# One of seven products in a weight product, split once more, in a two-layer cross-attention kernel

## The chip, the core and the metric

The kernel runs on one core of a Trainium2 chip. The metric is the device time of one execution in microseconds (us), lower being better. In the profile the core's engines are PE (matrix multiplication; PEld is its weight load), DVE (elementwise work and reductions), ACT (one function per element, here mostly copies, scaled copies and exponentials), POOL (here mostly the issue of transfers that add to their destination) and SP (the issue of plain loads). PE multiplies `lhs.T @ rhs` into banks of PSUM; everything else lies in SBUF. Each engine works through its own instructions in order and waits for the others by semaphores.

## The reference

Two cross-attention layers, one after the other, on `x` (8 x 100 x 1024) with a context of 8 x 1444 x 512. The first layer is, in essence:

```python
Q = query @ Wq + bq
K = key @ Wk + bk
V = key @ Wv + bv
weights = softmax(Q @ K.T / sqrt(1024))
x = query + (weights @ V) @ Wo + bo
```

The second layer has the same queries, keys and values with weights of its own, no output projection, and a layer norm on the sum. Everything is in float32.

## The kernel before

The scores `Q K.T` are rearranged so that the context is never projected: `Wq Wk.T` is one matrix of 1024 x 512, made first; the queries are multiplied by it, and the result meets the context directly. Likewise `Wv Wo` is one matrix. Each of the three weight products (`qk0` and `vo0` for the first layer, `qk1` for the second) is made by `weight_products`, with its sum over 1024 rows. The order is `qk0`, `vo0`, the first layer's queries, `qk1`, then the attention of the eight batches, twice.

`weight_products` cuts both factors into 2 x 2 blocks and makes the product of blocks by seven products in place of eight: sums of blocks are made first (S1 to S4 of the left factor, T1 to T4 of the right one), and the seven results are added into the four blocks of the output. With A and B for the blocks, the seven are: A11 B11 and A12 B21; S1 T1 (the variable Y); S2 T2, which goes on in the banks of A11 B11 (X); A22 T4 (W); S3 T3, again on X's banks; and S4 B22. In `qk0` each is 16 matmuls of 128 x 128 weights and 256 columns: four chunks of rows, each in two banks of PSUM with two blocks of columns. `inner_product` does the same once more inside one of the seven: seven smaller products of 4 matmuls with 128 columns. In `qk0` the last of the seven (`Q`) is made like that, and alternated with the one before it; `half_steps` gives the matmuls of a product one at a time, so that two can be taken in turn. In `vo0` and `qk1` (the variable `deep`) the product S1 T1 is split too, and alternated with S2 T2.

Values move by three helpers. `put` copies banks of PSUM to the output block by ACT. `add` adds a bank to it by DVE. `combine` makes the sums of blocks by DVE, one instruction for each of four chunks. Several of the sums overwrite their inputs: in `qk0` S2 is written over S1, and S3 over A21. The banks of X are copied out for block (0, 1) after S2 T2, before S3 T3 goes on in them.

PE's order is the order of the program, written out by hand. The other engines' orders come from a scheduler, except for instructions marked to stay in the order of the program; `vector.in_order = True` marks DVE's.

Beside the product each stage makes two bias vectors. `accumulate(0)` makes `bk`'s product with the left factor, 1024 wide, as a sum of eight terms, one for each chunk of rows. For `qk0`, `transferred_sum` makes the first four terms as scaled copies by ACT (`scaled_copies`, line 633) and adds them up in pairs by adding transfers that POOL issues (`transfer_added`, line 628). The second four are made by DVE in one tile, `prob1`, by one scaling and three multiply-adds (`second_half`), and a transfer adds the tile. `accumulate(1)` makes `bq`'s product with the right factor, 512 wide, by eight instructions of DVE.

The inputs of all weight products lie in a pool of ten tiles (`unit`). `vo0` needs eight of them, and only two are free during `qk0`, so SP's loads for `vo0` from its third on wait until a tile of `qk0` is read for the last time. The tiles `prob0` to `prob2` and the tiles of tags `row`, `wT` and `gT` are shared by the stages as room for sums.

Of the kernel before, what the change touches and what calls it, by code (L numbers as in the profile page):

```python
# [25 lines left out]
F32 = mybir.dt.float32  # L26
AF = mybir.ActivationFunctionType
ALU = mybir.AluOpType
# [3 lines left out]
P = 128  # L32
# [25 lines left out]
def two_layer_cross_attention(ctx: ExitStack, tc: tile.TileContext, a: dict, out: bass.AP):  # L58
# [32 lines left out]
    def wide_sums(name):  # L91
        return work.tile([P, LC, GT], F32, tag="gT", name=name, bufs=3).rearrange("p c t -> p (c t)")
# [70 lines left out]
    def half_steps(banks, lhs, rhs, fresh, nb, width):  # L163

        lhs, rhs = singles(lhs), singles(rhs)
        per = nb // len(banks)
        for i in range(len(lhs)):
            for n in range(nb):
                nc.tensor.matmul(  # L169
                    banks[n // per][:, n % per * width : (n % per + 1) * width],  # L170
                    lhs[i][:, n * P : (n + 1) * P],
                    rhs[i],
                    start=(fresh and i == 0 and n % per == 0),
                    stop=(i == len(lhs) - 1),
                    skip_group_check=True,
                )
                yield
# [8 lines left out]
    def combine(to, x, y, op, engine=vector):  # L186
        for t, p, q in zip(to, x, y):
            engine.tensor_tensor(t, p, q, op)
# [164 lines left out]
    def weight_products(name, left, right, l_width, r_width, scaled, between=None):  # L353
# [32 lines left out]

        accs = {}

        def accumulate(side):
            for v, of in scaled:  # L390
                if of != side:
                    continue
                width = (l_width, r_width)[side]
                first = 0 if side == 0 else l_width
                srcs = [(units[h][:, first : first + width], cols[v][:, h : h + 1]) for h in range(EC)]
                if width == E:
                    accs[v] = transferred_sum(f"{name}_{v}", srcs, name)
                    continue
                acc = work.tile([P, L], F32, tag="half", name=f"{name}_{v}", bufs=1)
                accs[v] = acc  # L400
                if early:
                    tiles = [acc] + [t[:, i * L : (i + 1) * L] for t in prob for i in range(2)]
                    scaled_sum(tiles + [weight_rows(f"{name}_{v}_7")[:, :L]], srcs)
                    continue
                for h, (src, by) in enumerate(srcs):
                    if h == 0:
                        vector.tensor_scalar(acc, src, by, None, ALU.mult)
                    else:
                        vector.scalar_tensor_tensor(acc, src, by, acc, ALU.mult, ALU.add)
# [20 lines left out]
        def pair(n):  # L430
            return [(bank2 if n == "w" else bank)(f"{name}_{n}{j}") for j in range(2)]

        def product(banks, lhs, rhs, fresh):
            half_product(banks, lhs, rhs, fresh, nb, rh)

        def block(r, c, j):

            n = r * nb + j * per
            return dst[:, n : n + per, c * rh : (c + 1) * rh]

        def put(r, c, banks):
            for j in range(2):
                nc.scalar.copy(block(r, c, j), banks[j].rearrange("p (n w) -> p n w", n=per))  # L443

        def add(r, c, banks):
            for j in range(2):
                to = block(r, c, j)
                vector.tensor_tensor(to, to, banks[j].rearrange("p (n w) -> p n w", n=per), ALU.add)
# [47 lines left out]
        if name == "qk0":  # L496

            t2, t4 = (weight_rows(f"{name}_t{n}") for n in (2, 4))
            T2, T4 = ([t[:, i * rh : (i + 1) * rh] for i in range(H)] for t in (t2, t4))
            Z = pair("z")  # L500
            product(Z, A12, B21, True)
            combine(T2, B22, T1, ALU.subtract)
            combine(T4, B21, T2, ALU.subtract)
            combine(S1, A21, A22, ALU.add)
            add(0, 0, Z)
            accumulate(1)
            W = pair("w")
            product(W, A22, T4, True)
            accumulate(0)
            put(1, 0, W)  # L510
        elif not deep:
            combine(S1, A21, A22, ALU.add)
            Z = pair("z")
            product(Z, A12, B21, True)
            accumulate(0)
        t = wide_sums(f"{name}_t")
        if deep:

            T2, S2, T4 = B11, A11, B21
            first, rest = slice(0, H - 1), slice(H - 1, H)  # L520
            combine(S1[first], A21[first], A22[first], ALU.add)
            for some in (first, rest):
                if some is rest:
                    combine(S1[some], A21[some], A22[some], ALU.add)
                combine(B12[some], B22[some], B12[some], ALU.subtract)
                combine(T2[some], B22[some], T1[some], ALU.subtract)
            Z = pair("z")
            product(Z, A12, B21, True)
            next(side, None)
            combine(A21, A11, A21, ALU.subtract)  # L530
            combine(S2, S1, A11, ALU.subtract)
            V = half_steps(X, S2, T2, False, nb, rh)
            for n, _ in enumerate(inner_product(f"{name}_y", S1, T1, nb, rh, t[:, 768:1536], *parts(1, 1))):
                run(islice(V, 2 * nb // (2 if n == 1 else 4)))
                if n == 1:
                    add(0, 0, Z)
                elif n == 3:
                    combine(T4, B21, T2, ALU.subtract)
                if n > 2:
                    next(side, None)  # L540
            run(V)
            put(0, 1, X)
        else:
            Y = pair("y")
            product(Y, S1, T1, True)
            put(1, 1, Y)
            vector.in_order = name != "qk0"
            combine(B12, B22, B12, ALU.subtract)
            if name != "qk0":
                T2, T4 = B11, B21  # L550
                combine(T2, B22, T1, ALU.subtract)
                add(0, 0, Z)
            combine(S1, S1, A11, ALU.subtract)
            S2 = S1
            combine(A21, A11, A21, ALU.subtract)
            if name != "qk0":
                combine(T4, B21, T2, ALU.subtract)
            product(X, S2, T2, False)
            put(0, 1, X)
        vector.in_order = True  # L560
        if name == "qk0":
            accs[scaled[0][0]][1]()
        V = half_steps(X, A21, B12, False, nb, rh)
        _, more = parts(0, 1)

        def last():
            combine(A12, A12, S2, ALU.subtract)
            if deep:
                for j in range(2):
                    to = block(0, 1, j)  # L570
                    vector.tensor_tensor(to, to, block(1, 1, j), ALU.add)
            else:
                add(0, 1, Y)
            return inner_product(f"{name}_q", A12, B22, nb, rh, t[:, 768:1536], more, more)

        if name == "qk0":
            run(islice(V, 2 * nb))
# [21 lines left out]
    def transferred_sum(name, srcs, of):  # L599

        n = EC if of == "qk1" else EC // 2
        tiles = [row(f"{name}_{n}") for n in range(2)] + [weight_rows(f"{name}_2")[:, :E]]
        tiles += [t[:, :E] for t in prob]
        if of != "qk0":
            tiles += [weight_rows(f"{name}_{n}")[:, :E] for n in range(6, 8)]
        if of == "qk1":
            tiles = [tiles[i] for i in (0, 3, 1, 4, 2, 5, 6, 7)]  # L610
        scaled_sum(tiles[:n], srcs[:n])

        def second_half():
            t = tiles[n]
            if of != "qk0":
                scaled_sum(tiles[n:], srcs[n:])
            else:
                for i, (src, by) in enumerate(srcs[n:]):
                    if i == 0:
                        vector.tensor_scalar(t, src, by, None, ALU.mult)  # L620
                    else:
                        vector.scalar_tensor_tensor(t, src, by, t, ALU.mult, ALU.add)
            transfer_added(tiles[0], t)

        return tiles[0], second_half

    def transfer_added(to, t):
        nc.gpsimd.dma_start(out=to, in_=t, accum_op=ALU.add)
# [6 lines left out]
    def scaled_sum(tiles, srcs, levels=None):  # L635

        scaled_copies(tiles, srcs)
        k = 1
        while k < len(tiles) and (levels is None or k < 2**levels):
            for i in range(0, len(tiles) - k, 2 * k):  # L640
                transfer_added(tiles[i], tiles[i + k])
            k *= 2
# [1032 lines left out]
```

## Time and profile before

| What | us |
|---|---|
| median of three runs | 574.87 (574.80 to 577.21) |
| the profiled execution | 574.70 |
| its span, first to last instruction | 572.8 |
| first matmul of `qk0` to the last | 4.57 to 52.35 |
| matmuls of `vo0` | 52.49 to 98.39 |
| DVE's last idle time before `qk0`'s sums | 8.5 to 13.41 |
| one 128x1024 scaled copy on ACT | 1.13 |
| one 128x1024 multiply-add on DVE | 1.28 |
| issue of an adding transfer on POOL | 0.86 to 0.91 |

The span is what the profiler saw between the first and the last instruction; the execution's time has 1.9 us more around it. Lines of a timeline give the start and the length of a group of instructions in us, then the engine, the line of the kernel, the operation, the tile written and the tiles read, the shapes and the count; in square brackets stands the engine's idle time before the group, and what ended it. Tiles that differ by a number in their names are put together, so `qk` stands for the inputs and the output of a query/key product, `qk_x` for X's banks, `qk_L_xattn_bk` for rooms of the key bias. In the table of stretches each engine has its busy time and its count of instructions; the last three columns are PE's granted clock, the share of the 16 DMA engines that was busy, and GB/s. In the shares of DMA queues q0 carries the transfers that POOL issues, q1 the loads that SP issues, each with packets, MB and its share of the 16 engines' time.

### The profile page before, as it was taken

What the parts mean: (1) busy time and instruction counts of PE and PEld (TensorE: products, weight loads), DVE (VectorE), ACT (ScalarE), POOL (GpSimd) and SP (SyncE); (2) the same over time, 40 slices, a digit from 0 to 9 for tenths busy, and PEclk for the clock granted to TensorE, in tenths of its full rate; (3) what the DMA queues carried; (4) which work ended last, traced back from release to release, by engine and by line L of the source; (5) the groups of instructions that cost most, each with busy time, mean ns of one, the idle gap of its engine ahead of it and who ended that gap; (6) DMA issues with size and microseconds to landing.
All of it is one profiled execution on the core that took longest, in us unless ns stands there. A gap on an engine that the chain in (4) does not pass through costs nothing.

```text
span 572.8 us, 17296 instructions
## 1 busy us (share of the span) xinstructions
PE 561.9 (98%) x7316; PEld 470.5 (82%) x7316; DVE 447.5 (78%) x1035; ACT 146.0 (25%) x383; POOL 112.9 (20%) x171
## 2 busy tenths in 40 slices
PE   9999999999999999999999999999999999999995
PEld 8887567678999999998997856678999869859672
DVE  1997979879989794876368687896688779979865
ACT  1331321356020112211111000123333035336633
POOL 3110110223100042242222000000421312404232
PEclk9999999999999999999999999999999999999999
DMA  8959979949929998999998003985799989985804
GB/s 283 315 112 327 313 191 291 317 85 206 208 57 348 378 353 323 355 374 340 333 355 275 3 1 141 280 291 189 233 311 305 314 265 330 311 261 168 211 15 92
DMA packets 73389, 141.23 MB, mean 247 GB/s; under 512 B 8160, under 2 KB 29920, under 8 KB 73312
## 3 DMA queue, kind: packets, MB, share of 16 engines
q1 hardware_dynamic: 66592, 121.40, 61.8%
q0 software_dynamic: 6288, 18.20, 16.3%
q8 instruction: 58, 0.95, 0.7%
q10 hardware_dynamic: 432, 0.52, 0.3%
q14 instruction: 19, 0.16, 0.1%
HBM read 123.49 MB, written 6.03 MB: 226 GB/s over the span
## 4 chain that ended last, share of the span: by engine, by line
PE 95%; issue 2%; DVE 1%; POOL 1%; ACT 1%; DVEq 0%; POOLq 0%
PE s L1076 22%; PE A L1004 21%; PE qk_x L169 7%; PE g_x L169 6%; PE vo_x L169 4%; PE o_x L169 3%; PE g_y L169 3%; PE o_x L1327 3%; PE qk_z L169 2%; PE o_y L1327 2%; PE o_y L169 1%; PE qk_w L169 1%; PE qk_y L169 1%; PE vo_z L169 1%; PE qk_q_x L169 1%
## 5 line engine op out<-in xcount | busy, mean ns | idle before, releaser
L1004 PE MATMUL A<-w,c 128*64 128x100 f32 (+2 forms) x3072 | 217.9, 250 | 1.0 <-issue 1.0
L1004 PEld LDWEIGHTS A<-w,c 128*64 128x64 f32 (+2 forms) x3072 | 191.6, 137 | 4.8 <-issue 2.8
L1076 PE MATMUL s<-g0T,cT 128*64 128x100 f32 (+1 forms) x1472 | 109.3, 250 | 1.3 <-issue 1.3
L1076 PE MATMUL s<-g1T,cT 128*64 128x100 f32 (+1 forms) x1472 | 109.6, 249 | 0.0
L1076 PEld LDWEIGHTS s<-g0T,cT 128*64 128x64 f32 (+1 forms) x1472 | 95.5, 136 | 1.7 <-issue 1.4
L1076 PEld LDWEIGHTS s<-g1T,cT 128*64 128x64 f32 (+1 forms) x1472 | 95.3, 136 | 1.1 <-DMA cT<-in_ctxT 0.6
L1294 POOL TENSOR_TENSOR part<-w 128x500 f32<-128x500 f32 x16 | 25.3, 1582 | 238.5 <-DVE rtotal L101 75.8
L1272 ACT ACTIVATE w<-w,negmax 128x100 f32<-128x100 f32 x96 | 34.9, 365 | 44.8 <-DVE negmax L101 44.5
L1140 ACT ACTIVATE w<-w 128x400 f32<-128x400 f32 (+2 forms) x32 | 12.7, 446 | 116.8 <-DVE w L101 106.1
L101 DVE STREAM_TRANSPOSE z<-xT 32x256 f32<-32x256 f32 x88 | 38.3, 436 | 1.4
L169 PE MATMUL qk_x<-qk 128*128 128x256 f32 x160 | 37.8, 380 | 0.0
L169 PEld LDWEIGHTS qk_x<-qk 128*128 128x128 f32 x160 | 28.9, 191 | 3.4 <-ACT qk L443 0.2
L1057 DVE RECIPROCAL rrow<-A 128x100 f32<-128x100 f32 x8 | 6.1, 767 | 23.9 <-PE A L1048 23.9
L169 PE MATMUL vo_x<-vo 128*128 128x512 f32 x48 | 23.3, 594 | 0.0
L101 DVE TENSOR_REDUCE most<-s 128x100 f32<-128x400 f32 (+1 forms) x24 | 12.5, 524 | 10.9 <-PE s L1076 10.4
L101 DVE SCALAR_TENSOR_TENSOR w<-s,kb 128x400 f32<-128x400 f32 (+2 forms) x32 | 14.1, 463 | 8.2 <-PE s L1076 7.8
L101 DVE TENSOR_TENSOR w<-w,rtotal 128x400 f32<-128x400 f32 (+2 forms) x32 | 18.1, 567 | 1.1
L1272 ACT ACTIVATION_READ_ACCUMULATOR w<-w,negmax 128x1 f32 x96 | 17.9, 187 | 0.0
L739 ACT ACTIVATE g1T<-g_x,k 128x400 f32<-128x400 f32 x4 | 2.4, 593 | 60.5 <-PE g_x L169 60.3
L1297 POOL TENSOR_TENSOR part<-part 128x100 f32<-128x100 f32 x32 | 15.8, 493 | 2.5
L101 DVE TENSOR_TENSOR qk<-qk 128x256 f32<-128x256 f32 (+2 forms) x26 | 14.4, 580 | 0.0
L169 PE MATMUL qk_z<-qk 128*128 128x256 f32 x64 | 14.1, 379 | 0.0
(484 smaller groups left out, 1001.1 us busy)
## 6 DMA issues: line engine op xcount, KB each, us to landing
c<-in_ctx SPq DMA_DIRECT2D x176, 256.0 KB, 5.7
cT<-in_ctxT SPq DMA_DIRECT2D x96, 176.0 KB, 4.9
cT<-in_ctxT SPq DMA_DIRECT2D x32, 370.0 KB, 6.2
cT<-in_ctxT SPq DMA_DIRECT2D x32, 352.0 KB, 6.1
cT<-in_ctxT SPq DMA_DIRECT2D x32, 194.0 KB, 5.5
vo<-in_L_xattn_Wo SPq DMA_DIRECT2D x8, 512.0 KB, 9.1
qk<-in_L_xattn_WqT SPq DMA_DIRECT2D x8, 512.0 KB, 5.8
qk<-in_L_xattn_WqT SPq DMA_DIRECT2D x15, 256.0 KB, 5.3
```

What stands on the lines that cost most here:

```text
L101: ins = getattr(nc.vector, op)(*args, **kw)
L169: nc.tensor.matmul(banks[n // per][:, n % per * width : (n % per + 1) * width], lhs[i][:, n * P : (n + 1) * P], rhs[i], start=(fresh and i ...
L739: nc.scalar.activation(dst[g][:, c, :], banks[j][:, :GT], AF.Identity, bias=u[:, c : c + 1])
L1004: nc.tensor.matmul(ps[h * HP : (h + 1) * HP, k * T : (k + 1) * T], block[rows, m % CQ, k * P + h * HP : k * P + (h + 1) * HP], s["w"][rows ...
L1057: nc.vector.reciprocal(r, ps[:, GT : GT + T])
L1076: nc.tensor.matmul(to, cT[k][:, o : o + n], q[:, k, t0 : t0 + T], start=(k == 0 and m % GM == 0), stop=(k == LC - 1 or (k == LC - 2 and no ...
L1140: nc.scalar.activation(rows, rows, AF.Exp)
L1272: ins = nc.scalar.activation(rows[:, i, :], rows[:, i, :], AF.Exp, bias=negmax[:, i : i + 1], accum_out=total[:, i : i + 1])
L1294: add(part, w[:, 0:5, :], w[:, 5:10, :], ALU.add)
L1297: add(part[:, 0, :], part[:, 0, :], more, ALU.add)
L1327: nc.tensor.matmul(ps[:n, :], lhs[0][:, i, :], rhs[0][:, i, :], start=(fresh and i == 0), stop=(i == 1), skip_group_check=True,)
```

## The change

In `qk0` the product S1 T1 is now made by `inner_product`, as in the other two stages, and its steps alternate with the matmuls of S2 T2: two of the 16 after each of the seven steps, four after the second. For this S2 is no longer written over S1, but into two tiles of tag `gT`, and the last product's sums get a third one. DVE keeps the order of the program from here on. The result of S1 T1 goes to block (1, 1) in parts, by `put` and `add`; where it was added to block (0, 1) from PSUM, the finished block (1, 1) is now added.

`accumulate(1)` is cut in two: its first four terms stay where they were, the second four come after the fifth small product, between the difference for T3 and the one for S3.

The second four terms of the key bias are now four scaled copies by ACT, in three steps that are set off during the small products, and adding transfers: the fifth term into `prob1` (t) and the sixth into `prob2` (u), u added to t; the seventh into `prob0` (v); the eighth into u again; then u added to v, v to t, and t to the sum of the first four. That is seven adding transfers in all, where there were four.

```diff
-        def accumulate(side):
+        def accumulate(side, some=range(EC)):
...
-                acc = work.tile([P, L], F32, tag="half", name=f"{name}_{v}", bufs=1)
-                accs[v] = acc
+                if some[0] == 0:
+                    accs[v] = work.tile([P, L], F32, tag="half", name=f"{name}_{v}", bufs=1)
+                acc = accs[v]
...
-                for h, (src, by) in enumerate(srcs):
+                for h in some:
+                    src, by = srcs[h]
...
-            accumulate(1)
+            accumulate(1, range(H))
             W = pair("w")
             product(W, A22, T4, True)
             accumulate(0)
             put(1, 0, W)
...
         else:
-            Y = pair("y")
-            product(Y, S1, T1, True)
-            put(1, 1, Y)
-            vector.in_order = name != "qk0"
-            combine(B12, B22, B12, ALU.subtract)
...
-            combine(S1, S1, A11, ALU.subtract)
-            S2 = S1
-            combine(A21, A11, A21, ALU.subtract)
...
-            product(X, S2, T2, False)
-            put(0, 1, X)
+            vector.in_order = True
+            late = accs[scaled[0][0]][1]()
+            rooms = [wide_sums(f"{name}_s2_{i}") for i in range(2)]
+            S2 = [t2[:, i * lh : (i + 1) * lh] for t2 in rooms for i in range(2)]
+            combine(S2, S1, A11, ALU.subtract)
+            Y = inner_product(f"{name}_y", S1, T1, nb, rh, t[:, 768:1536], *parts(1, 1))
+            V = half_steps(X, S2, T2, False, nb, rh)
+            for n, _ in enumerate(Y):
+                run(islice(V, 2 * nb // (2 if n == 1 else 4)))
+                if n in (1, 2, 5):
+                    next(late)
+                if n == 3:
+                    combine(B12, B22, B12, ALU.subtract)
+                elif n == 4:
+                    accumulate(1, range(H, EC))
+                    combine(A21, A11, A21, ALU.subtract)
+            run(V)
+            put(0, 1, X)
         vector.in_order = True
-        if name == "qk0":
-            accs[scaled[0][0]][1]()
...
         def last():
             combine(A12, A12, S2, ALU.subtract)
-            if deep:
-                for j in range(2):
-                    to = block(0, 1, j)
-                    vector.tensor_tensor(to, to, block(1, 1, j), ALU.add)
-            else:
-                add(0, 1, Y)
-            return inner_product(f"{name}_q", A12, B22, nb, rh, t[:, 768:1536], more, more)
+            for j in range(2):
+                to = block(0, 1, j)
+                vector.tensor_tensor(to, to, block(1, 1, j), ALU.add)
+            room = t if deep else wide_sums(f"{name}_q_t")
+            return inner_product(f"{name}_q", A12, B22, nb, rh, room[:, 768:1536], more, more)
...
         def second_half():
...
+            scaled_sum(tiles[n:], srcs[n:])
+            transfer_added(tiles[0], tiles[n])
+
+        def second_half_in_turn():
+            t, u, v = tiles[n], tiles[n + 1], tiles[n - 1]
+            scaled_copies((t, u), srcs[n : n + 2])
+            transfer_added(t, u)
+            yield
+            scaled_copies((v,), srcs[n + 2 : n + 3])
+            yield
+            scaled_copies((u,), srcs[n + 3 :])
+            for to, src in ((v, u), (t, v), (tiles[0], t)):
+                transfer_added(to, src)
+            yield
+
+        return tiles[0], second_half_in_turn if of == "qk0" else second_half
```

More of the change, by code (lines that the diff above doesn't have):

```diff
@@ L510, in weight_products @@
             put(1, 0, W)
[L511 to L515, printed above, removed]
         t = wide_sums(f"{name}_t")
@@ L543, in weight_products @@
         else:
-            Y = pair("y")
-            product(Y, S1, T1, True)
-            put(1, 1, Y)
-            vector.in_order = name != "qk0"
-            combine(B12, B22, B12, ALU.subtract)
[L549 to L552, printed above, removed]
-            combine(S1, S1, A11, ALU.subtract)
-            S2 = S1
-            combine(A21, A11, A21, ALU.subtract)
-            if name != "qk0":
-                combine(T4, B21, T2, ALU.subtract)
-            product(X, S2, T2, False)
+            vector.in_order = True
[15 more added lines that the diff above has]
+            run(V)
             put(0, 1, X)
         vector.in_order = True
-        if name == "qk0":
-            accs[scaled[0][0]][1]()
         V = half_steps(X, A21, B12, False, nb, rh)
@@ L613, in second_half @@
         def second_half():
[L614 to L625, printed above, removed]
+            scaled_sum(tiles[n:], srcs[n:])
[12 more added lines that the diff above has]
+        return tiles[0], second_half_in_turn if of == "qk0" else second_half
     def transfer_added(to, t):
```

## The prediction, made before the changed kernel ran

> **What bounds the kernel now.** I read the page's head first, then what PE waited for, then the timeline of the first 60 us engine by engine, and last the DMA shares, one us at a time.
>
> ```profile
> span 572.8 us, 17296 instructions
> PE 561.9 (98%) x7316; PEld 470.5 (82%) x7316; DVE 447.5 (78%) x1035; ACT 146.0 (25%) x383; POOL 112.9 (20%) x171
> ...
> PE warm L113 <- DVE ones L110: 1.1, 1, 1.1
> PE A L1004 <- issue: 1.0, 3, 0.5
> ```
>
> PE is busy for 98% of the span, and its list of waits adds up to under 4 us, so no wait later on can absorb a delay: what is added to PE early comes out at the end, and what is taken off PE is gained. In the first layer's query/key product PE runs without a gap:
>
> ```profile
> 25.30 7.07 PE L169 MATMUL qk_y<-qk_s 128*128 128x256 f32 x32
> 32.20 7.07 PE L169 MATMUL qk_x<-qk_t,qk_s 128*128 128x256 f32 x32
> 39.11 3.70 PE L169 MATMUL qk_x<-qk 128*128 128x256 f32 x16
> 42.64 1.05 PE L169 MATMUL qk_q_x<-qk 128*128 128x128 f32 x8
> 43.53 3.62 PE L169 MATMUL qk_x<-qk 128*128 128x256 f32 x16
> ```
>
> Each line is a start, a length and a group; a matmul leaves two records, so x32 is 16 matmuls. The line at 25.30 is the product that the change splits, the one at 32.20 the next it is alternated with. The line at 39.11 accumulates into the same two banks that the one at 32.20 filled, so each bank must have been copied out by ACT first. ACT and POOL around it:
>
> ```profile
> 38.45 0.58 ACT L443 COPY qk<-qk_x 128x512 f32<-128x512 f32 x1 [5.46 <-PE qk_x L169]
> 39.31 0.59 ACT L443 COPY qk<-qk_x 128x512 f32<-128x512 f32 x1 [0.28 <-PE qk_x L169]
> ...
> 25.61 0.88 POOL L628 DMA_DIRECT2D qk_L_xattn_bk<-prob  x1 [1.16 <-ACT prob L633]
> 32.69 0.86 POOL L628 DMA_DIRECT2D qk_L_xattn_bk<-qk_L_xattn_bk  x1 [6.20 <-DMA qk_L_xattn_bk<-prob]
> 37.75 0.86 POOL L628 DMA_DIRECT2D qk_L_xattn_bk<-prob  x1 [4.21 <-DVE qk L101]
> ```
>
> The copy at 38.45 ends at 39.03 and PE goes on at 39.11: that copy is already on the edge of the path. POOL issues the key bias' adding transfers in order; the one at 32.69 had to wait for the one at 25.61 to land.
>
> **The change, part by part.** Base: the profiled execution took 574.70 us, its span 572.8 and 1.9 around it; the median of the runs shown is 574.87, 0.17 above.
>
> *1. The split product.* Out go 16 matmuls of 256 columns: 25.30 to 32.20 is 6.90 us, 0.43 each. In come 7 x 4 of 128 columns. The last product has this form already: its neighbours start 0.89 apart (qk_q_z at 46.99, qk_q_y at 47.88, qk_q_x at 48.77), so 7 x 0.89 = 6.25. Gain 0.65: both products would end at 25.30 + 6.25 + 6.91 = 38.46, not 39.11.
>
> *2. The sums for it, on DVE.* Added: sums of 128x256 (0.34 each, pairs of 0.75 starting 0.67 apart) and of 128x128 (pairs 0.41 apart). Four of each pair is 4.3 us, four adds from PSUM 1.3, and the adds of one block to another replace two adds from PSUM at 0.6 each. Taken off DVE: the second half of the key bias, 0.66 + 3 x 1.20 = 4.3. I laid DVE's built order out by these steps from 21.03, where the first sum of A21 and A22 starts now. S2, in rooms of its own, is whole at 25.9; the first small sums at 28.1 (PE's third small product needs only the first pair of them, 27.0, and starts at 29.7); the second set at 29.2 (needed 31.4), the third at 30.6 (needed 33.2), A21 at 37.0 (needed from 38.5). I cost this at nothing: the cover is the product itself, with 1.5 to 2.6 us of slack, and without it each us late would be a us on PE.
>
> *3. The key bias' second half on ACT.* Four scaled copies of 128x1024; three of that form now take 3.23 us, 1.05 each. The first two go into two rooms as soon as ACT is free (26.8 to 28.9), the third into the room of the transfer issued at 25.61 (landed 32.1), 33.2. The small products' copies between them are needed no earlier than 34.9. But the fourth needs the room of the second, which must first have been added to the first by a transfer, and POOL has that transfer behind the one at 32.69. In ACT's built order the fourth stands *ahead* of the two copies of qk_x, and ACT works in order. When does that transfer land?
>
> ```profile
> 33.00:34.00 1.00, 1.00 (x7) 0.87 (x6) 1.00 (x3) 0.00 (x0) 0.54 (x1) 1.00 0.00 0
> 34.00:35.00 1.00, 1.00 (x6) 0.88 (x5) 1.00 (x2) 0.00 (x0) 0.00 (x0) 1.00 1.02 197
> 35.00:36.00 1.00, 1.00 (x6) 0.89 (x5) 1.00 (x2) 0.00 (x0) 0.00 (x0) 1.00 1.04 197
> 36.00:37.00 1.00, 1.00 (x7) 0.87 (x6) 1.00 (x2) 0.00 (x0) 0.00 (x0) 1.00 0.71 131
> 37.00:38.00 1.00, 1.00 (x6) 0.90 (x5) 1.00 (x3) 0.00 (x0) 0.25 (x1) 1.00 0.00 0
> ```
>
> The last two columns are the DMA engines' share and GB/s. One transfer of 512 KB, issued at 32.69, keeps all 16 engines full from 34.0 to 36.7 at 197 GB/s, with nothing beside it, and lands at 37.2 (the list of issues gives 4.5 us). The next one can be issued at 33.6 but moves only after it: 36.7 + 2.7 = 39.4, landed about 39.9. Then the fourth scaled copy to 40.95, the qk_x copy to 41.55, and PE goes on at 41.6, 2.5 later than now (3.15 later than part 1 would let it). Bounds: with no lag after the last byte and a quick copy 41.2, +2.1; with the 7.2 us that a transfer took when issued at 42.28, landing at 40.8, +3.4.
>
> The Trainium skill (DMA: Bandwidth & Descriptors, Anatomy of one DMA) gives a transfer about 2.0 us and its bytes at 436 GB/s; by that both would have landed by 37.1, PE would resume at 38.8, and this term would be -0.3. The row above has less than half that rate for an adding transfer, and the row decides.
>
> *4. What is queued behind.* The key bias now takes seven adding transfers where it took four; the last three stand on POOL in front of the second weight product's value-bias transfers (the first of these at 42.28 now). Weight loads for that product leave SP when PE and DVE release the buffers, from 41.16 now, so they move with PE, 2.5 later. What an adding transfer does to them:
>
> ```profile
> q0 software_dynamic: 40, 0.16, 86.7%
> q1 hardware_dynamic: 34, 0.07, 20.8%
> ...
> q1 hardware_dynamic: 154, 0.41, 104.8%
> ```
>
> The first two are the queues' shares from 46 to 47 us, with a transfer under way: loads move 0.07 MB. The last is 50 to 51, with none: 0.41. A transfer holds this for some 3.4 us (44.8 to 48.2), so it costs the loads about 0.8 x 3.4 = 2.7 us. Now two fall into their time (issued 42.28 and 53.28). After it, the first extra one is issued at 41.3 while the engines are idle; then the second extra one (about 46.3, when the first has landed), a value-bias one, the third extra (about 54) and a value-bias one follow: four. Two more are 5.3 us on the last load. Its landing now is 52.5 + 9.7 = 62.2; PE needs it for the fourth quarter of vo_z, 59.44 + 3 x 1.72 = 64.6, so 2.4 of slack. Added wait: 5.3 - 2.4 = 2.9. Bounds: 0, if one of the two falls behind the last load (2.7 against 2.4 of slack, rounded down); 5.3, if the earlier loads use the slack up first. I take 2.9 because the loads, stretched, run to about 69, after all four have been issued. ACT's copies of vo_x stand behind a scaled copy that waits for the second extra transfer (landed about 54): needed at 61, hidden. The bias' end itself is wanted by DVE at 89.9 only, and lands near 63.
>
> Sum: 574.70 + 2.5 + 2.9 = 580.1, and with the 0.17 to the median **580.2**.
>
> **The rivals.** *Only the first wait.* The loads have room enough, since the first extra transfer runs while the engines idle and the lag of a transfer behind loads (4.5 us from issue at 53.28 to its first byte at 57.8) pushes the third out of the way. 574.87 + 2.1 to 3.4: 577.0 to 578.3. Against it: POOL's order has both extra ones ahead of the value bias' third.
>
> *Faster.* The second of the two transfers lands by 36.6, because two in flight share better than one after the other; the fourth scaled copy then ends by 37.7 and only part 1 is left: 574.87 - 0.65 = 574.2. It decides from a landing at 36.6 on; every us later is a us on PE. Against it: 16 engines full at 197 GB/s, and 1 MB in all.
>
> *Worse.* The loads of vo are starved in a row and each quarter of vo_z waits afresh, with DVE's sums behind the last one: 2.5 + over 5.3, 583 to 587. For it: loads spread unevenly over the engines (the list has 8.5 us for the load issued at 43.25, while two later ones were already moving). Against it: the value-bias transfers of now would also come later, out of their way.
>
> **How the numbers follow.** Forecast (both waits, 578.3 to 583) 0.57; only the first wait 0.24; faster 0.07; worse 0.12. The range goes from the first wait at its low bound with no second, 574.7 + 2.1 = 576.8, to both at their high ones, 574.7 + 3.4 + 5.3 = 583.4. A measurement of this kernel tells 0.5%, 2.9 us, from no change: slower than that is above 577.7, which takes the forecast, the worse case and some third of the first-wait case, 0.77; the gain of 0.65 is within it, as is the rest, 0.21; 0.02 is left for a gain that I don't see.
>
> **What would show it.** After: PE with a gap near 38.5 of some 3 us, ended by ACT's copy of qk_x; ACT idle until about 39.9, ended by a transfer between prob rooms, then one 128x1024 copy, then qk_x. Seven key-bias transfers on POOL. vo loads' first issue at 43.7 in place of 41.16, and PE waiting for a load of Wo in vo_z, near 66 to 70. The small products 0.89 apart. The forecast is wrong if the qk_x copy starts by 38.4, if vo_z has no gap, or if a gap stands inside the alternated pair, which would mean that DVE's cover in part 2 was not there.

## The result, and the profile after

The changed kernel took 584.77 us (median of 6 runs, 581.91 to 588.28) beside 575.3 us for the kernel before on the same chip (6 runs, 573.91 to 577.21): a ratio of 1.0161, 95% interval 1.013 to 1.0191. It is slower by some 9.5 us. The prediction had the sign and the two waits, but 580.2 us, and its range ended at 583.4. The time lies where its rival "worse" stood (583 to 587).

The head of the page of the changed kernel:

```profile
span 584.0 us, 17383 instructions
PE 564.7 (97%) x7340; PEld 471.6 (81%) x7340; DVE 448.9 (77%) x1051; ACT 150.7 (26%) x389; POOL 115.9 (20%) x174
```

PE's share falls from 98% to 97%, and the span is 11.2 us longer with 2.8 us more of PE busy: most of the loss is PE standing still (work at a lower clock counts as busy here). Its list of waits (engine, line, who ended the wait: us in total, times, longest):

```profile
PE A L1003 <- issue: 3.9, 5, 1.5
PE vo_z L169 <- DMA vo<-in_L_xattn_Wo: 2.8, 2, 2.5
PE qk_x L169 <- ACT qk L445: 2.6, 1, 2.6
PE warm L113 <- DVE ones L110: 1.1, 1, 1.1
PE g_x L169 <- DMA g_t<-xT: 0.7, 1, 0.7
```

Three entries are new: a wait for a copy of ACT's in qk_x, a wait for loads of Wo in vo_z, and a short one in the queries. The first line is in the traces of both kernels, and differs from trace to trace (1.0 us in the one of before, 2.2 in two later ones of the changed kernel). The timeline of PE shows where the two large ones stand:

```profile
35.87 1.05 PE L169 MATMUL qk_y_y<-qk_s 128*128 128x128 f32 x8
36.76 1.03 PE L169 MATMUL qk_x<-qk_t,qk_s 128*128 128x256 f32 x4
37.63 1.05 PE L169 MATMUL qk_y_x<-qk_s 128*128 128x128 f32 x8
38.52 1.03 PE L169 MATMUL qk_x<-qk_t,qk_s 128*128 128x256 f32 x4
42.17 3.72 PE L169 MATMUL qk_x<-qk 128*128 128x256 f32 x16 [2.63 <-ACT qk L445]
...
62.53 3.60 PE L169 MATMUL vo_z<-vo 128*128 128x512 f32 x8
66.38 1.95 PE L169 MATMUL vo_z<-vo 128*128 128x512 f32 x4 [0.25 <-DMA vo<-in_L_xattn_Wo]
70.84 3.43 PE L169 MATMUL vo_z<-vo 128*128 128x512 f32 x4 [2.51 <-DMA vo<-in_L_xattn_Wo]
74.07 1.32 PE L169 MATMUL vo_y_x<-vo_s 128*128 128x256 f32 x4
```

A small product and its share of the next alternate without a gap, 0.89 and 0.87 apart. Then PE stops for 2.63 us in front of the group at 42.17, and for 2.76 in vo_z. The last quarter of vo_z also takes 3.43 us where the same four records at 66.38 take 1.95. ACT around the first wait, and POOL's issues:

```profile
35.21 0.37 ACT L462 COPY qk<-qk_y_w 128x256 f32<-128x256 f32 x1 [1.03 <-PE qk_y_w L169]
40.50 1.15 ACT L632 ACTIVATE prob<-qk,L_xattn_bk 128x1024 f32<-128x1024 f32 x1 [4.92 <-DMA prob<-prob]
41.56 1.05 ACT L445 COPY qk<-qk_x 128x512 f32<-128x512 f32 x2
```

```profile
33.25 0.86 POOL L627 DMA_DIRECT2D qk_L_xattn_bk<-qk_L_xattn_bk  x1 [6.18 <-DMA qk_L_xattn_bk<-prob]
33.79 1.20 POOL L627 DMA_DIRECT2D prob<-prob  x1
41.94 0.86 POOL L627 DMA_DIRECT2D prob<-prob  x1 [6.95 <-ACT prob L632]
48.48 0.86 POOL L627 DMA_DIRECT2D prob<-prob  x1 [5.68 <-issue]
49.02 1.20 POOL L627 DMA_DIRECT2D vo_L_xattn_bv<-vo_L_xattn_bv  x1
57.04 0.86 POOL L627 DMA_DIRECT2D qk_L_xattn_bk<-prob  x1 [6.82 <-DVE qk L101]
58.04 0.86 POOL L627 DMA_DIRECT2D vo_L_xattn_bv<-prob  x1
```

ACT stands for 4.92 us until the adding transfer between two prob rooms has landed, makes the eighth term's scaled copy, and only then copies qk_x, which PE waits for. On POOL the second half's last three transfers (41.94, 48.48, 57.04) have one of the value bias' among them (49.02) and one right behind (58.04). The shares of the queues of the changed kernel between 63 and 64 us, with a transfer under way:

```profile
q0 software_dynamic: 36, 0.15, 73.6%
q1 hardware_dynamic: 36, 0.10, 28.2%
```

All loads together move 0.10 MB in that microsecond. And the clock in vo_z of the changed kernel, us by us (behind the window: summed busy time, then PE, PEld, DVE, ACT, POOL, the granted clock of TensorE, DMA share, GB/s):

```profile
70.00:71.00 1.00, 0.16 (x1) 0.16 (x2) 0.08 (x1) 0.18 (x1) 0.78 (x2) 1.00 1.05 400
71.00:72.00 1.00, 1.00 (x2) 0.48 (x3) 1.00 (x2) 0.97 (x1) 0.96 (x2) 0.62 1.06 405
72.00:73.00 1.00, 1.00 (x2) 0.34 (x1) 1.00 (x4) 0.00 (x0) 0.73 (x1) 0.50 1.05 400
73.00:74.00 1.00, 1.00 (x2) 0.34 (x1) 1.00 (x4) 0.00 (x0) 0.12 (x1) 0.50 1.07 394
74.00:75.00 1.00, 1.00 (x4) 0.80 (x3) 1.00 (x4) 0.00 (x0) 0.00 (x0) 0.67 1.18 315
```

PE works through all of 71 to 75 us, but at half the clock for most of it: 3.23 us from 70.84 to 74.07 in place of 1.72, and 0.3 more in the next line.

By stages of PE's timeline (from the first group of qk_x, from bb_ps, and from u<-u_sums, each to the next, and the last to wqbk):

| kernel | weights of qk | weights of vo | queries | first product |
|---|---|---|---|---|
| before | 47.78 | 46.04 | 36.27 | 6.91 |
| changed | 50.81 | 51.01 | 37.25 | 7.78 |

The last column, a part of the first stage, is the time from the first qk_x to the first qk_z, ahead of everything that the change touches.

### The profile page after: what moved, and what is told of

It reads as the page before. It is cut to its first block, busy times and chain, and to the rows that moved or that the text cites. A ratio compares the mean times of both kernels' runs of the same rounds, so it can differ in the third digit from the quotient of the medians.

```text
span 584.0 us, 17383 instructions
## 1 busy us (share of the span) xinstructions
PE 564.7 (97%) x7340; PEld 471.6 (81%) x7340; DVE 448.9 (77%) x1051; ACT 150.7 (26%) x389; POOL 115.9 (20%) x174
## 4 chain that ended last, share of the span: by engine, by line
PE 81%; DMA 9%; DVE 3%; issue 3%; ACT 1%; SPq 1%; POOL 1%; POOLq 0%; DVEq 0%; ACTq 0%
PE s L1075 22%; PE A L1003 21%; PE qk_x L169 5%; PE g_x L169 5%; PE o_x L169 3%; PE o_x L1326 3%; DMA qk<-in_L_xattn_WqT 3%; DMA vo<-in_L_xattn_Wo 2%; PE vo_x L169 2%; DMA g_t<-xT 2%; PE g_y L169 2%; PE o_y L1326 2%; PE o_y L169 1%; DVE vo L101 1%; PE qk_z L169 1%
## 5 line engine op out<-in xcount | busy, mean ns | idle before, releaser
L1139 ACT ACTIVATE w<-w 128x400 f32<-128x400 f32 (+2 forms) x32 | 12.7, 446 | 119.3 <-DVE w L101 108.6
L101 DVE SCALAR_TENSOR_TENSOR w<-s,kb 128x400 f32<-128x400 f32 (+2 forms) x32 | 14.1, 464 | 8.2 <-PE s L1075 7.8
L101 DVE TENSOR_TENSOR qk<-qk 128x256 f32<-128x256 f32 (+2 forms) x28 | 15.6, 587 | 0.0
L169 PE MATMUL qk_z<-qk 128*128 128x256 f32 x64 | 14.1, 379 | 0.0
```

What stands on the lines that cost most here:

```text
L101: ins = getattr(nc.vector, op)(*args, **kw)
L169: nc.tensor.matmul(banks[n // per][:, n % per * width : (n % per + 1) * width], lhs[i][:, n * P : (n + 1) * P], rhs[i], start=(fresh and i ...
L1139: nc.scalar.activation(rows, rows, AF.Exp)
```

## The experiments

Medians and ratios are each against runs of the kernel before made beside them (medians of 576.21 us for e1 to e4, 576.23 for f1 to f4, 576.05 for f5 and f6, 575.52 for f7 and f8). A ratio is not exactly that of the two medians. Each experiment has one trace, of one of its runs.

**1. The order on ACT: e1_copies_first.** The changed kernel with the eighth term's scaled copy behind the two copies of qk_x.

```diff
-                if n in (1, 2, 5):
+                if n in (1, 2):
                     next(late)
...
             put(0, 1, X)
+            next(late)
```

> The changed kernel with one step moved: the eighth term of the key bias is issued after the two copies of qk_x, not ahead of them. Theory (two causes that add): the gap on PE between the alternated pair and the next product (2.6 us in the changed kernel) falls under 0.3, but the seven adding transfers stay, so PE still waits in vo_z, 2 to 5 us of it; the time falls by 2 to 3 us only, to 4 to 8 us over before. Rival (one cause: ACT's late copy delays everything behind it, the loads too): vo_z has no wait either, and the time is within 1 us of before. Rival (the loads alone matter, the first gap would be made up for later): the time does not fall by more than 1 us.

Measured: 587.98 us (585.85 to 589.17), ratio 1.0207 [1.018, 1.0233]: more than the changed kernel's, where 4 to 8 us over before were expected. The first wait is gone (the stage takes 47.12, a gain of 0.66 on the kernel before, as costed for the split). The wait in vo_z, which was expected to stay with the seven transfers, is gone too. In its place VectorE stands for loads of Wv, which it didn't before, and PE for VectorE:

```profile
58.41 0.43 DVE L101 TENSOR_TENSOR vo_s<-vo,vo 128x256 f32<-128x256 f32 x1 [1.86 <-DMA vo<-in_L_xattn_WvT]
60.32 0.43 DVE L101 TENSOR_TENSOR vo_s<-vo,vo 128x256 f32<-128x256 f32 x1 [1.48 <-DMA vo<-in_L_xattn_WvT]
```

```profile
67.72 1.10 PE L169 MATMUL vo_x<-vo 128*128 128x512 f32 x2 [1.15 <-DVE vo L101]
```

The vo stage is 1.5 us longer than before. Neither the theory nor the first rival fits that: late loads don't need the late copy, but the number of transfers doesn't settle what they cost. The main loss stands in the queries, 47.83 us in place of 36.27: a wait of 9.98 us and 1.6 us of half clock behind it. POOL's issues and PE's wait in e1_copies_first:

```profile
87.58 0.86 POOL L628 DMA_DIRECT2D prob<-vo_L_xattn_bv  x1 [13.84 <-DMA vo_L_xattn_bv<-vo_L_xattn_bv]
97.09 0.86 POOL L628 DMA_DIRECT2D vo_L_xattn_bv<-prob  x1 [8.65 <-DMA qk<-in_L_xattn_WkT]
97.63 1.64 POOL L628 DMA_DIRECT2D g_t<-xT  x1
```

```profile
116.80 1.70 PE L169 MATMUL g_z_x<-g_t,g_t 128*128 128x200 f32 x4 [9.98 <-DVE g_t L101]
```

The queries' own adding transfer (g_t<-xT) has its input from ACT at 89.6, but POOL stands in front of it with the value bias' last two, each waiting for the one before, and issues it at 97.63. So the first wait is the order on ACT; and taking it away isn't worth its 2.6 us, since the transfers then fall otherwise on the same queue (experiment 5 looks into this).

**2. The number of transfers: e2_fewer_transfers, and both together: e3_both.** e2 is the changed kernel without two of the second half's four transfers (the key bias lacks its last two terms); e3 has this and the order of e1.

```diff
-            for to, src in ((v, u), (t, v), (tiles[0], t)):
+            for to, src in ((tiles[0], t),):
```

> The changed kernel without two of the seven adding transfers (the eighth term onto the seventh, and these onto the fifth and sixth): the seventh and eighth terms are missing from the key bias. ACT's order and its wait stay. Theory: the gap of about 2.6 us ahead of the product after the alternated pair stays, vo_z has no wait for a load over 0.3 us and no stretch at half clock; 4.5 to 6.5 us less than the changed kernel, 2 to 4 us over before. Rival (one cause, the late copy): vo_z still waits, less than 1.5 us gained. Rival (the loads are late only because their buffers come free later): the same, under 1.5 us gained.

> Both edits of the two runs before at once (the seventh and eighth terms of the key bias are missing). Theory: both waits gone, and what is left is the gain of the split product, 0.65 us under before, 573.5 to 575.5. If the split product or its sums on DVE cost something themselves, it is over before by 1 us or more, with a gap inside the alternated pair.

Measured: e2 580.17 us, 1.0075 [1.0051, 1.01], as expected. The first wait stays (2.32 us, with 1.7 us of half clock behind it), the one in vo_z is gone, and the vo stage is at 46.06, the 46.04 of the kernel before. e3 577.1 us (12 runs), 1.0023 [1.0004, 1.0042], over the 573.5 to 575.5 expected: no wait in either stage, 47.26 and 46.06. So each of the two waits has the cause that the prediction named, with the place of the transfers among the loads counting beside their number (e1), and together with what hangs on them they are nearly the whole loss. That e3 isn't faster, although its first stage is 0.52 shorter, is read in the queries. The second transfer of g_t and the product that needs it, in the kernel before:

```profile
104.17 1.28 POOL L628 DMA_DIRECT2D g_t<-xT  x1 [13.61 <-ACT g_t L795]
114.44 5.54 PE L169 MATMUL g_x<-g_t,g_s 128*128 128x400 f32 x16
```

and in e3_both:

```profile
104.71 1.28 POOL L628 DMA_DIRECT2D g_t<-xT  x1 [14.60 <-ACT g_t L795]
115.55 5.61 PE L169 MATMUL g_x<-g_t,g_s 128*128 128x400 f32 x16 [0.95 <-DMA g_t<-xT]
```

Before, the transfer issued at 104.17 landed at 113.9 and PE took it up without a wait at 114.44: this chain through ACT, POOL and the DMA engines had 0.5 us to spare. In e3 the queries begin 0.44 us earlier, but the first transfer of g_t, issued 0.45 earlier, takes 14.0 us to land where it took 13.0; so the second one is issued 0.54 later and itself takes 10.7 in place of 9.7. PE waits, and what the split gained is lost (the queries take 37.90 in place of 36.27). Why these transfers take longer isn't shown.

**3. The bias on VectorE again, with the split kept: e4_bias_on_dve.** One scaled copy on ACT and three multiply-adds on VectorE, one transfer, so four for the key bias as before. In a part of the edit that isn't shown, the last product begins four steps later.

```diff
-            scaled_copies((t, u), srcs[n : n + 2])
-            transfer_added(t, u)
+            scaled_copies((t,), srcs[n : n + 1])
             yield
...
+            for src, by in srcs[n + 1 :]:
+                vector.scalar_tensor_tensor(t, src, by, t, ALU.mult, ALU.add)
+                yield
+            transfer_added(tiles[0], t)
```

> The split product kept, the key bias' second half in one tile again (its first term by ACT, three by DVE), with the four transfers of before; all but the last four matmuls of the product after the pair come ahead of the last product, so that DVE has time. Nothing is left out. Theory: no gap at the pair's end over 0.3 us, no wait in vo_z, 573.5 to 576. Rival (DVE's sums for the split product are the cost): 1 to 3 us over before, with PE waiting for DVE in the last product.

Measured: 578.07 us (12 runs, 576.74 to 579.89), 1.0036 [1.0015, 1.0056], over the 573.5 to 576 expected. Most of the loss goes with the transfers and the order on ACT, and the split by itself brings nothing here either. The rival has a part in it: the steps of the last product start up to 1.11 us apart in place of 0.89, 0.6 us in all, which is the split's gain. PE also waits 0.3 for VectorE in vo_x and 0.9 in the queries.

**4. The dose: f1_two_extra_transfers and f2_three_extra_transfers.** The kernel *before*, with two or three adding transfers between tiles of 512 KB put in behind the key bias' last one.

```diff
+    nc.gpsimd.memset(prob[2][:, :E], 0.0)
...
             accs[scaled[0][0]][1]()
+            for _ in range(2):
+                transfer_added(prob[2][:, :E], prob[1][:, :E])
```

> The kernel before, with two adding transfers more (512 KB each, from one tile of VectorE's into a third tile that nothing reads before it is filled anew), issued by GpSimd behind the key bias' last one, so that they move while the vo stage's weights are loaded. Nothing is left out, and neither TensorE's nor ScalarE's nor VectorE's order is touched. Theory (the transfers take the DMA engines from the loads): vo_z waits for a load of Wo for 2 to 4 us, some 579 to 581.5 us. Rival (the late loads come from buffers freed late in the changed kernel, not from the number of transfers): no wait in vo_z, within 1 us of the kernel before.

> The same with three transfers more instead of two. Theory: each transfer costs the loads 2 to 3 us, once the slack is gone, so that this is 2 to 3 us above the kernel with two (581 to 584 us). Rival: within 1 us of the kernel before, and no difference between the two kernels.

Measured: 580.23 us, 1.0057 [1.0041, 1.0073], and 581.52 us, 1.0089 [1.007, 1.0108]. PE's waits in f1 and in f2:

```profile
PE vo_z L170 <- DMA vo<-in_L_xattn_Wo: 1.7, 1, 1.7
...
PE vo_x L170 <- DVE vo L101: 1.3, 1, 1.3
```

```profile
PE vo_z L170 <- DMA vo<-in_L_xattn_Wo: 3.6, 1, 3.6
```

The wait of the changed kernel appears in the old one by the transfers alone, with the split left out: the rival (buffers freed late) falls as the only cause. In f1 PE waits for VectorE in vo_x besides, which had stood 5.8 us for loads of Wv. Two transfers cost 4.0 us between the medians, 3.3 by the ratio. The third adds 1.9 to the wait in vo_z, but only 1.3 to the median (1.8 by the ratio), less than the 2 to 3 expected: f2 has 1.7 us of half clock behind its wait, but no wait for VectorE in vo_x.

**5. What stood in front of the queries: f3_copies_first_less_bias.** e1 without one transfer of the value bias.

```diff
-            scaled_sum(tiles[n:], srcs[n:])
+            scaled_sum(tiles[n:], srcs[n:], None, ((0, 2),))
...
             for i in range(0, len(tiles) - k, 2 * k):
-                transfer_added(tiles[i], tiles[i + k])
+                if (i, k) not in skipped:
+                    transfer_added(tiles[i], tiles[i + k])
```

> The changed kernel with ScalarE's copies of the first pair of sums ahead of the eighth scaled copy (as in e1_copies_first), and with the value bias' sum cut: the transfer that adds terms 6 and 7 to terms 4 and 5 is left out, so that the value bias lacks these two terms. Theory (the 10 us wait in the queries of e1_copies_first came from the queries' transfer standing behind the value bias' ones on GpSimd's queue): the wait shrinks by about what one such transfer holds the queue (5 us or more), 578 to 583 us. Rival (the wait is for VectorE's or ScalarE's own work in the queries, which the order of copies moved): the wait stays near 10 us, 587 us or more.

Measured: 579.17 us (12 runs, 576.0 to 582.62), 1.0049 [1.0029, 1.0069]; the trace is of the fastest of the 12. POOL in f3:

```profile
90.12 1.30 POOL L627 DMA_DIRECT2D g_t<-xT  x1 [15.90 <-ACT g_t L793]
```

Now the transfer goes as soon as ACT has its input, PE has no wait in the queries, and they take 36.27 again. So e1's 10 us came from what stood ahead on POOL: the transfer was issued 8.0 us after its input was there, and then took 15.9 us to land, against 12.7 here. The wait of PE for VectorE in vo_x is there as in e1 (1.29 us).

**6. The half clock: f4_kept_busy, f5_kept_busy_in_vo_z, f6_changed_again, f7_kept_busy_in_both, f8_changed_third.** f4, f5 and f7 are the changed kernel with matmuls on constants where PE waits; f6 and f8 are the changed kernel itself. The core of the edit of f7 (f4 has ten at the first place and ten ahead of vo_z's last quarter; f5 only the two fives):

```diff
+    def keep_busy(n):
+        ps = bank("busy")
+        for _ in range(n):
+            nc.tensor.matmul(ps[:, :P], ones, ones, start=True, stop=True)
...
             put(0, 1, X)
+            keep_busy(12)
...
-            product(Z, A12, B21, True)
+            steps = half_steps(Z, A12, B21, True, nb, rh)
+            run(islice(steps, 2 * nb))
+            for _ in range(2):
+                if name == "vo0":
+                    keep_busy(5)
+                run(islice(steps, nb))
+            run(steps)
```

> The changed kernel with ten matmuls of 128x128 on constants, into a spare bank, where TensorE waits for the copies in qk_x, and ten more ahead of vo_z's last quarter; nothing is left out. Theory (behind an idle stretch of some 2.5 us the clock is granted at half for about 4 us, which costs 1.7 to 1.9 us): no window of the first two stages below a clock of 0.9, and 1 to 2 us less than the changed kernel (582.5 to 584 us). Rival (the half clock is no part of the loss): 584 to 586 us, no difference from the changed kernel that can be measured.

> The changed kernel with five matmuls of 128x128 on constants, into a spare bank, ahead of vo_z's third quarter and five ahead of its fourth, the places where TensorE waits for the loads of Wo (the earlier ten stood behind the wait); nothing is left out. They take 1.2 us each five by f4_kept_busy's rows and lie in a wait of 2.2 to 2.8 us. Theory (TensorE's clock is halved behind the idle stretch, 1.7 to 1.9 us): no window of the vo stage below a clock of 0.9, and 1 to 2 us less than the changed kernel beside it. Rival (kept busy or not, the clock falls there or the time comes back later): within 0.7 us of the changed kernel.

> The changed kernel itself, for a comparison on the same chip and for a second trace. All theories: 583 to 586 us. In the trace, what belongs to the change is there again (the wait of some 2.6 us in qk_x, the waits for Wo's loads in vo_z, the later transfer in the queries); what was chance is not (theory: the first product's 0.9 us at the very start; rival: it comes back and belongs to the change).

> The changed kernel with matmuls of 128x128 on constants in both places where TensorE waits: twelve (some 2.9 us by f4_kept_busy's rows) ahead of the copies' wait in qk_x, where it stood idle for 2.6 to 3.7 us, and five and five in vo_z; nothing is left out. Theory (one of the two idle stretches halves the clock in each run, at 1.7 us for a drop of 3.4 us and 3.0 us for one of 6.5 us, as seen in qk_x of f5_kept_busy_in_vo_z and f6_changed_again): no window of the first two stages below 0.9 (a stretch of under 2 us left idle), qk_x's group of 16 in 3.7 us, and 1.5 to 3 us less than the changed kernel beside it. Rival (the half clock only stands in the time that the loads take anyway, so that a later wait takes its place): no half clock, yet within 0.7 us of the changed kernel.

> The changed kernel itself beside f7_kept_busy_in_both, and its third trace. Theory: 584 to 587 us, and the clock at 0.50 behind one of the two waits again, a few us long. Rival (the two drops seen were chance): no drop in this one, and 583 us or less.

Measured: f4 584.02 us, 1.0144 [1.0112, 1.0175]; f5 585.63, 1.0157 [1.012, 1.0194]; f6 586.56, 1.0189 [1.0156, 1.0221]; f7 585.09, 1.0152 [1.0119, 1.0186]; f8 584.87, 1.0161 [1.013, 1.0192].

f4 settles nothing about the price: PE stood for 2.24 us ahead of vo_z's *third* quarter, the second ten came after that, and the half clock was there all the same. In f5 the half clock was gone from vo_z and stood in qk_x, behind the wait that had no filler. The same place in f6:

```profile
42.51 6.75 PE L169 MATMUL qk_x<-qk 128*128 128x256 f32 x16 [3.73 <-ACT qk L445]
49.10 1.05 PE L169 MATMUL qk_q_x<-qk 128*128 128x128 f32 x8
```

The group of 16 takes 3.72 us in the first trace of the changed kernel, 5.41 in e2 and f5, and 6.75 here: 1.7 and 3.0 us lost. f8, the third trace of the changed kernel, has the same two waits without it:

```profile
41.64 3.72 PE L169 MATMUL qk_x<-qk 128*128 128x256 f32 x16 [1.73 <-ACT qk L445]
...
70.48 1.98 PE L169 MATMUL vo_z<-vo 128*128 128x512 f32 x4 [2.79 <-DMA vo<-in_L_xattn_Wo]
```

With fillers in both places, f7:

```profile
39.05 2.84 PE L356 MATMUL busy<-ones 128*128 128x128 f32 x24
41.73 3.62 PE L169 MATMUL qk_x<-qk 128*128 128x256 f32 x16
...
68.15 1.96 PE L169 MATMUL vo_z<-vo 128*128 128x512 f32 x4 [1.46 <-DMA vo<-in_L_xattn_Wo]
69.94 1.28 PE L356 MATMUL busy<-ones 128*128 128x128 f32 x10
71.05 1.88 PE L169 MATMUL vo_z<-vo 128*128 128x512 f32 x4
```

Every row is at full speed and the clock is 1.00 in each window read. But the median is that of f8: the theory's 1.5 to 3 us are not there. The trace is of the fastest of f7's six runs, 581.12 us; the other five took 583.9 to 586.6 at mean clocks of 0.993 to 0.998, so whether the fillers kept the clock up in them isn't known. The fillers themselves cost about 1.4: the second five run for 1.1 us (69.94 to 71.05), with no wait behind them, so the loads were there, and the twelve hold PE some 0.3 longer than ACT's copy would (in the first trace PE goes on 0.61 us after that copy starts; here it started at 40.81). And f8's trace has no half clock, against what was expected of it, so the changed kernel doesn't always pay it. What speaks for its price is the 18 runs of the changed kernel: the five with a mean clock of 0.993 or less took 586.8 us on average, the five with 0.996 or more 583.8; a run that waits longer may lose both ways, so this doesn't part the clock from the wait. So the half clock is shown in the rows of two of three traces, at 1.8 and 3.0 us; that removing it makes the kernel faster is not shown.

The three traces of the changed kernel against the one of before, less the difference in the first product. That one trace, at 574.70 us, is 0.6 to 1.5 under the later medians of its kernel, so a term can be off by some tenths:

| term, us | predicted | first | f6 | f8 |
|---|---|---|---|---|
| qk stage without half clock (wait less the split's gain) | +2.5 | 2.2 | 3.3 | 1.3 |
| waits for Wo's loads in vo_z | +2.9 | 2.8 | 1.7 | 2.8 |
| half clock behind one of the two | 0 | 1.8 | 3.0 | 0 |
| vo_x waiting for VectorE, and the rest of the vo stage | 0 | 0.4 | 1.8 | 1.2 |
| queries | 0 | 1.0 | 0.2 | 0.8 |
| sum | +5.4 | 8.1 | 10.0 | 6.1 |

VectorE and PE behind the fourth row, in f6:

```profile
69.06 0.42 DVE L101 TENSOR_TENSOR vo_s<-vo,vo 128x256 f32<-128x256 f32 x1 [4.89 <-DMA vo<-in_L_xattn_WvT]
```

```profile
77.04 1.10 PE L169 MATMUL vo_x<-vo 128*128 128x512 f32 x2 [1.15 <-DVE vo L101]
```

Expected of the first product was that its 0.9 us are chance. It took 6.91 us in the trace of before, 7.78, 7.17 and 8.15 in the three of the changed kernel, but 6.91 in f4, which has the change, and 7.51 and 7.43 in f1 and f2, which don't have it. It doesn't belong to the change.

## Why the prediction was wrong in its size

*Part 1, the split product: right.* The small products start 0.89 apart, and where nothing waits behind them (e1, f3) the stage is 0.66 shorter, against 0.65 costed.

*Part 2, VectorE's sums at nothing: right.* The pair runs without a gap. f6 and f8 have PE waiting 1.15 and 0.35 for VectorE in vo_x, but VectorE itself had stood there for loads of Wv, 4.89 us in f6 and 2.50 in f8, and f1 has the same wait without the split: it belongs to part 4.

*Part 3, the first wait of +2.5: right in mechanism and size.* The three traces have 2.2, 3.3 and 1.3, 2.3 on the mean; e1 shows the cause. Nothing came of the faster rival. Nor did the -0.3 come that the prediction worked out from the Trainium skill (DMA: Bandwidth & Descriptors, Anatomy of one DMA): the second transfer, issued at 33.79, held ACT until 40.50.

*Part 4, +2.9 for loads behind two more transfers: right in mechanism, and near in size* (2.8, 1.7, 2.8 in vo_z; two times 2.7 is 5.4, not 5.3, a slip of 0.1), with e2 taking it away and f1 bringing it into the old kernel. The transfers were issued at 41.94, 48.48 and 57.04, for 41.3, 46.3 and 54 predicted. It looked only at the last load of Wo: late loads of Wv reach PE too, through VectorE in vo_x. The rival "only the first wait" falls. "Worse" has the number but not the way: vo_z waits once or twice, 1.7 to 2.8 us in all, not afresh in each quarter for over 5.3.

*The step that failed is the sum,* 574.70 + 2.5 + 2.9: it took a wait to cost its own length and nothing behind it. Three things were left out. The clock is granted at half behind an idle stretch of this length in some runs, which is 1.6 us on the mean of three traces and up to 3.0. The rest of the vo stage loses 0.4 to 1.8 us, of which VectorE's late sums in vo_x are 1.15 in f6 and 0.35 in f8. And nothing was put down for the queries, which lost 0.2 to 1.0: their g_t transfers had 0.5 us to spare before. In all three traces the first of them is issued 9.13 us ahead of the stage, as in the kernel before (9.12), so it isn't held up on POOL as in e1. But in the first trace the second one takes 11.6 us to land in place of 9.7, and in f8 the first one 14.1 in place of 13.0. What slows them is open, and f4 and f7, with the same change, lose nothing there (36.27). Together the three put the mean of the sums at 8.0 for 5.4, although the two waits themselves came out smaller than predicted.

The base was low besides: 574.87 was the median of three runs, and the five later ones are 575.3 to 576.2. What is left of the 9.4 to 10.5 us between the medians, above the 8.0, has no cause shown. In the traces it stands in the first product and behind the product s<-g0T, 181 to 194 us into the span: from there all these kernels run the same work, yet it takes 390.2 to 393.7 us from trace to trace, 391.4 in the one of before, 393.6, 392.8 and 393.7 in the three of the changed kernel, but 390.2, 391.7 and 391.0 in f4, f5 and f7, which have the change.

No run points to a version that beats the kernel before: the split is worth 0.65 us where it stands, and e3 and e4, which are free of both waits, lose that again, e3 (which leaves out two terms) in the queries, e4 in the last product, in vo_x and in the queries.

## What to carry to other kernels

Work moved from a busy engine to idle ones still goes through their queues: price the transfers it adds by what they take from the loads beside them (here 1.3 to 2 us of the whole time for each of 512 KB), and follow each queue to the next stage's transfer behind it (e1). Look at every load that comes late, also at one that reaches PE only through another engine. A forecast wait of 2 to 4 us on TensorE should carry a term for the clock behind it, and a chain with half a microsecond to spare downstream can take back a small gain ahead of it (e3). Waits are not independent: removing the first one here moved the transfers and opened a wait of 10 us.

## What the runs showed of the hardware

TensorE's granted clock fell to 0.50 behind listed waits of 2.24 us (f4), 2.32 (e2), 2.51 (changed), 3.17 (f5), 3.55 (f2), 3.73 (f6) and 9.98 (e1), and not behind 1.73 (f1 and f8), 2.01 (f5, in vo_z), 2.63 (changed, in qk_x) and 2.79 (f8): between 2.24 and 2.79 us both happened, and behind the four longer ones it always fell. By the windows' clock it stayed low for about 3.4 us in five of these traces, 6.8 in f6 and 10.2 in e1, which is one, two and three times 3.4. The Trainium skill (TensorE: Matmul & The Clock Gate, What's actually happening) has the clock drop after at least one idle window of about 3.4 us, and the windows run free of the program. The lengths of the low spells agree with steps of such a window, but three of the drops came behind a listed wait of 2.24 to 2.51 us, shorter than one window.

An adding transfer of 512 KB takes most of the DMA engines' time from the loads beside it: with one under way its queue has 73.6% and the loads 28.2%, and they move 0.10 MB in the microsecond (63 to 64 us, changed kernel). In the kernel before, the prediction's rows have 0.07 MB with one under way and 0.41 without.
